# Two-layer attention on a picture: another order of the seven products, other halves of the channels, and a group norm by halves for the first batch

## The chip, the cores and the metric

The kernel runs on one core of a Trainium2 chip. Its time is device time in microseconds (us). TensorE (PE in the profile) multiplies matrices from SBUF into PSUM; VectorE (DVE), ScalarE (ACT) and GpSimd (POOL) work on whole tiles; SyncE (SP) issues most transfers. [...]

## The reference

The input is 8 pictures of 32 x 32 pixels with 512 channels, that is, per picture 1024 tokens of 512 values. Two layers follow each other, each with a residual:

```python
x = x + layer0(group_norm(x))   # 16 heads of 32: softmax(q k^T / sqrt(32)) v, then @ w_proj + b_proj
x = x + layer1(group_norm(x))   # 4 heads of 128: softmax((q k^T + position logits) / ...) v, then @ Wo
```

`group_norm` has 32 groups of 16 channels and takes mean and variance over a group's channels and all pixels. `layer0` gets q, k and v from one matrix w_qkv (512 x 1536), `layer1` from Wq, Wk and Wv (512 x 512 each). The position logits of layer 1 are products of q with two small tables of relative positions, one for the row and one for the column of a pixel, shifted so that each pair of pixels gets the logit of its distance. All is fp32.

## The kernel before, in words

**Tiling.** A picture's activations lie transposed in a `block` of SBUF: 128 partitions x 4 chunks of channels x 1024 tokens. `NB` = 512 tokens are a half (`NH` = 2), `NT` = 8 blocks of 128 tokens are the keys. PSUM has three pools: "ps" (4 banks, the scores of layer 0), "acc" (1), and "bank" with 3 buffers, which serve the products x, y, z, the position logits `pp`, and the scores and sums of layer 1.

**Projections.** Each of the eight 1024x512 by 512x512 projections per picture is Strassen's scheme in Winograd's form, with seven products instead of eight. The weights are cut into quarters (`quarter`, L120), the activations into a11, a12, a21, a22: the first index is the half of the tokens, the second the half of the channels. `forms` (L324 to L336) makes four sums on VectorE: s1 = a21 + a22 (L332), s2 = s1 - a11 (L333), s3 = a11 - a21 (L334, written over a21), s4 = a12 - s2 (L335). `Matrix.add_up` (L137, subtractions at L146) makes four such sums of the weights, once per matrix; `factor` (L152) names the weight that belongs to each product. `seven` (L341 to L396) runs the products; it is a generator that yields after each product. One call covers one unit (u = 0 or 1, a quarter of the 512 output columns in each half), so a projection is two units. In the list `fs` and in `ORDER` (L165) product number i is P(i+1):

```python
ORDER = [0, 5, 1, 4, 6, 2, 3]          # P1 P6 P2 P5 P7 P3 P4
return [a11, a12, s4, a22, s1, s2, a21]
```

P1 opens bank x and is copied by ACT (`p1`, L367). P6, which takes s2, opens y; DVE makes the snapshot a = y + p1 (L372). P2 adds onto x, which gives output quarter c11. P5 adds onto y, snapshot b = y + p1 (L380). P7, with s3, opens z and is copied by ACT (`p7`, L386). P3 adds onto y and gives c12; P4 adds onto z and gives c21, and c22 is b + p7. P5 can't start before a is read from y, nor P3 before b is. What becomes of the quarters is up to a sink: `Plain` (L398) writes them as q, k or v; `Onto` adds them onto the residual (L431, L436, L438) and, for the last projection, turns each finished block back (`ot`, L835) and sends it out (L840). `Stream` loads the weights of the next unit, product by product, on SyncE's queue, in the same queue as the outputs.

**Norm.** `statistics` (L241) takes mean and variance of a chunk into one small tile `mv`; `group_norm` (L254) turns it, averages over groups by a chain of some ten small DVE operations (L274 to L285), takes the power -0.5 on POOL (L289) and then scales four chunks (L292), yielding after the chain and after each second chunk.

**Attention.** `attention_0` (L519) goes over chunks m in the order 0, 2, 1, 3, halves h and key blocks j. A step is: scores into ps (L532), exp on ACT into one of two buffers `e` (L540), the product with v into acc (L551), and on DVE the addition of e onto `es` (L560 for the first, L562 after), which releases the e buffer. At the end of a half the sums over keys follow (L572) and `normalise` (L489): ACT copies su (L495), DVE turns it, takes reciprocals (L497 to L513), POOL multiplies (L517). `attention_1` (L637) does the same per head with its scores (L647), to which L648 adds the position logits from `posT`, in a bank; heads in order 0 to 3. `position_logits` (L594) makes posT in four steps: matmuls into `pp` (L608, L615), four ACT copies (L628) and four DVE subtractions (L633).

**What sets the order.** The program is written as generators, and they are merged by hand. In iteration b the steps of `attention_0` of picture b are interleaved with everything else (`side_by_side`, L862, which spreads a list of work by its cost over the attention's steps): the output projection of layer 0 for picture b-1 (`after_0`), the output projection of layer 1 for b-2 (`after_1`) with the norm of layer 1 for b-1, then `second` (L804: q, k, v of layer 1 and the position logits), `attention_1` of b-1 with the loading and norm of picture b+1, and `before_0` (q, k, v of layer 0 for b+1). `woven(main, side, start, gap, places)` (L850) inserts one step of `side` into `main` from step `start` on, at every `gap`. The norm of layer 1 is woven into `after_1` from product 3 at every third, the position logits into k and v from step 2, at three places per unit. A `hook` lets the four forms of the next output projection run inside the second unit of another projection, after its P3. In the first iteration there is no `after_1` to hide the norm of picture 0, so it runs with only attention beside it, each of its four steps with the cost ALONE. The last iterations have less and less work to merge, and after `attention_1` of picture 7 its output projection stands alone. A last few instructions (L979 to L985) set a flag if a softmax sum was out of bounds; another path of the program would then compute everything anew, which does not happen here.

## Time and profile before

Three runs took 3903.42, 3903.57 and 3906.62 us; the median is 3903.57 us. The profiled execution spans 3900.2 us. What matters in it:

| stretch of the span (us) | what runs | waits of TensorE of 0.25 us or more |
|---|---|---|
| 0 to 36 | loading, norm and first projection of picture 0 | 5.02 for x_rows, 9.32 for x_v, two short ones |
| 106 to 320 | attention_0 of picture 0 | eleven, together 13.5; three above 2 |
| 345 | output projection of picture 0 | 3.50 |
| 390 to 415 | norm of layer 1, picture 0 | 1.04, 7.58, 1.06, 1.04, 1.04 |
| 415 to 3200 | the iterations with full work | about 2.75 in each of five |
| 3214 to 3290 | last iteration with attention_0: output projections, norm | seven, together 7.6, the longest 2.66 |
| 3410 to 3460 | end of the last attention_0 | 0.40, 2.42, 2.58 |
| 3619 to 3866 | work of picture 6 and 7 that is left | 0.57, 1.74, 2.98, 0.32, 0.38, 0.75, 3.15 |
| 3890 to 3900 | outputs, flag | no matmul |

A row of the profile's groups names the line of the kernel, the engine, output and inputs, the number of instructions, their busy time and the mean of one, and then the idle time ahead of them with what ended it. A row of the waits names the waiting engine and line, then the releasing one, the total, how often and the longest. A stretch of the windows view gives busy time of each engine, and in PEclk the clock that was granted to TensorE, 1.00 being the full one; the mean over the run is 0.995.

### The profile page before, as it was taken

How to read it: one execution, taken by the hardware profiler on the slowest of the kernel's cores; microseconds unless marked ns; L12 is line 12 of the kernel's file. 1: busy time of each engine (PE TensorE's matmuls, PEld its weight loads, DVE VectorE, ACT ScalarE, POOL GpSimd, SP SyncE). 2: the span in 40 equal slices, each digit the busy share in tenths (PEclk: the TensorE clock that was granted, in tenths of full speed). 3: DMA queues.
4: the chain of work that ended last, by engine and by line, in shares of the span. 5: the costliest groups of instructions: out<-in, count | busy, mean ns of one | idle time of the engine just before them, and what ended most of it. 6: DMA issues, size and time to landing. Idle time of an engine off the chain costs nothing. (4 is left out here: it accounts for less than half of the span.)

```text
span 3900.2 us, 79833 instructions
## 1 busy us (share of the span) xinstructions
PE 3806.4 (98%) x34478; PEld 1370.9 (35%) x34478; DVE 2517.3 (65%) x2905; ACT 1725.1 (44%) x1767; POOL 621.7 (16%) x400
## 2 busy tenths in 40 slices
PE   8999899999999999999999999999999999999998
PEld 3222244232442224432343323433234332244353
DVE  5777675576745867468664686656865568754544
ACT  2554553445434454344544445344453445643132
POOL 1341001121101211012111121111210112011101
PEclk9999999999999999999999999999999999999999
DMA  5221120133202322023120241103311123110401
GB/s 172 86 95 51 40 61 3 39 117 70 59 5 63 107 57 55 12 91 84 46 55 17 92 94 40 44 24 97 88 45 32 31 92 69 32 63 18 124 17 23
DMA packets 482984, 234.73 MB, mean 60 GB/s; under 512 B 269600, under 2 KB 461376, under 8 KB 481600
## 3 DMA queue, kind: packets, MB, share of 16 engines
q1 hardware_dynamic: 470992, 213.74, 20.3%
q0 software_dynamic: 2608, 13.70, 1.0%
q8 instruction: 274, 4.49, 0.5%
q10 hardware_dynamic: 9024, 2.10, 0.3%
q14 instruction: 86, 0.70, 0.1%
HBM read 170.72 MB, written 58.72 MB: 59 GB/s over the span
## 5 line engine op out<-in xcount | busy, mean ns | idle before, releaser
L540 ACT ACTIVATE e<-ps 128x2048 f32<-128x2048 f32 x512 | 961.7, 1878 | 844.6 <-PE ps L532 605.9
L562 DVE TENSOR_TENSOR es<-es,e 128x2048 f32<-128x2048 f32 x384 | 890.8, 2320 | 400.2 <-ACT e L540 397.4
L532 PE MATMUL ps<-q,k 32*64 32x512 f32 x8192 | 577.2, 615 | 36.4 <-ACT e L540 36.3
L650 ACT ACTIVATE e<-ps 128x512 f32<-128x512 f32 x512 | 305.9, 598 | 585.9 <-PE ps L648 549.1
L551 PE MATMUL acc<-e,v 128*32 128x512 f32 x4096 | 547.1, 606 | 0.4 <-ACT su L495 0.4
L647 PE MATMUL ps<-q,k 128*128 128x512 f32 x1024 | 523.6, 593 | 0.4 <-DVE posT L633 0.4
L659 PE MATMUL acc<-e,v 128*128 128x512 f32 x1024 | 521.9, 592 | 0.0
L517 POOL TENSOR_TENSOR q<-q,su 128x512 f32<-128x512 f32 x128 | 214.3, 1674 | 1564.8 <-DVE su L513 1538.1
L670 DVE TENSOR_TENSOR es<-es,e 128x512 f32<-128x512 f32 x384 | 291.8, 760 | 264.0 <-ACT e L650 262.5
L648 PE MATMUL ps<-posT,sel 128*128 128x512 f32 x512 | 406.6, 794 | 0.0
L647 PEld LDWEIGHTS ps<-q,k 128*128 128x128 f32 x1024 | 193.6, 190 | 246.2 <-issue 240.6
L532 PEld LDWEIGHTS ps<-q,k 32*64 32x64 f32 x8192 | 120.4, 130 | 432.4 <-ACT e L540 217.0
L659 PEld LDWEIGHTS acc<-e,v 128*128 128x128 f32 x1024 | 193.1, 189 | 146.7 <-issue 105.0
L551 PEld LDWEIGHTS acc<-e,v 128*32 128x32 f32 x4096 | 81.5, 108 | 413.4 <-issue 365.8
L560 DVE TENSOR_TENSOR es<-e,e 128x2048 f32<-128x2048 f32 x64 | 174.7, 2730 | 39.7 <-ACT e L540 39.7
L497 DVE STREAM_TRANSPOSE tu<-su 128x512 f32<-128x512 f32 x128 | 90.6, 708 | 136.2 <-ACT su L495 136.0
L495 ACT COPY su<-sums 128x512 f32<-128x512 f32 x128 | 75.1, 586 | 151.3 <-PE sums L572 83.4
L648 PEld LDWEIGHTS ps<-posT,sel 128*128 128x128 f32 x512 | 97.3, 190 | 122.5 <-issue 122.5
L668 DVE TENSOR_TENSOR es<-e,e 128x512 f32<-128x512 f32 x64 | 44.2, 691 | 145.7 <-ACT e L650 145.7
L633 DVE TENSOR_TENSOR posT<-pp,posT 32x512 fp32r<-32x512 f32 x128 | 112.0, 875 | 32.2 <-ACT posT L628 30.8
L421 POOL TENSOR_TENSOR k<-b_k,p_k 128x512 f32<-128x512 f32 x32 | 51.2, 1599 | 477.0 <-ACT p_k L386 474.9
L628 ACT CAST posT<-pp 32x512 fp32r<-32x512 f32 x128 | 106.0, 828 | 45.2 <-PE pp L615 44.1
(195 smaller groups left out, 4510.1 us busy)
## 6 DMA issues: line engine op xcount, KB each, us to landing
w_qkv<-ws_qkv SPq DMA_DIRECT2D x168, 128.0 KB, 2.5
d<-x0T SPq DMA_DIRECT2D x32, 512.0 KB, 3.6
x1T<-d SPq DMA_DIRECT2D x32, 512.0 KB, 5.5
d<-x1T SPq DMA_DIRECT2D x32, 512.0 KB, 3.6
x2T<-d SPq DMA_DIRECT2D x32, 512.0 KB, 5.9
w_qkv<-in_L_conv_w_qkv SPq DMA_DIRECT2D x126, 128.0 KB, 2.2
out<-ot SPq DMA_DIRECT2D x240, 64.0 KB, 2.0
xs<-in_x SPq DMA_DIRECT2D x224, 64.0 KB, 2.6
```

Of the source, the lines that this page charges most:

```text
L517: nc.gpsimd.tensor_tensor(dst, dst, su, op=ALU.mult)
L532: nc.tensor.matmul(ps[some, r, :], k[m][rows, j * P + 64 * i : j * P + 64 * i + 64], q[m][rows, h * NB : (h + 1) * NB], start=True, stop=True,
L540: nc.scalar.activation(e, ps, AF.Exp, scale=D0 ** -0.5)
L551: nc.tensor.matmul(acc[r * D0 : (r + 1) * D0, :], v[:, j, c0 : c0 + D0], e[:, r, :], start=(j == 0), stop=(j == NT - 1),)
L560: nc.vector.tensor_add(state["esum"], state["first"], e)
L562: nc.vector.tensor_add(state["esum"], state["esum"], e)
L633: nc.vector.tensor_sub(rest, logits, greater)
L647: nc.tensor.matmul(ps, k[h][:, keys], q[:, h, queries], start=True, stop=False)
L648: nc.tensor.matmul(ps, sel_flat[:, keys], posT[:, h, queries], start=False, stop=True)
L650: nc.scalar.activation(e, ps, AF.Exp, scale=1.0 / math.sqrt(D1))
L659: nc.tensor.matmul(acc, v[:, j, h * D1 : (h + 1) * D1], e, start=(j == 0), stop=(j == NT - 1),)
L670: nc.vector.tensor_add(state["esum"], state["esum"], e)
```

## The change

The change aims at the places where a projection has to wait for the last piece of its input.

1. The halves of the channels are chunks 0, 2 and 1, 3 instead of 0, 1 and 2, 3 (activations and weight quarters alike). Since attention works in the order 0, 2, 1, 3, a11 and a21 are then complete when half of the chunks are. `attention_1` takes its heads in the same order.
2. The products run in the order P1, P7, P6, P2, P5, P4, P3. P7 needs only s3 = a11 - a21, which is now the first form and has a tile of its own; s1 is written over a21 instead. All three banks are open from P6 to P2. The quarter that is finished last is c12.
3. `forms_in_parts` is a generator. Hooks run one part each after P5, P4 and P3 of the second unit; before, all four forms ran in one hook.
4. The group norm takes a range of halves. For picture 0, layer 0 and layer 1, it runs by halves: the first half of the layer 1 norm is woven into the output projection, the second runs in the steps that cost ALONE. All other norms stay whole. They and the position logits are woven in one or two products later.
5. The weight sums of WQ0 and WK0 on DVE wait at the start for the last form of picture 0, and ACT does all copies of the turned input.

```diff
-        return w[:, k * HC : (k + 1) * HC, n * HN : (n + 1) * HN]
+        return w[:, k::2, n * HN : (n + 1) * HN]
+    IN_HALVES = [0, 2, 1, 3]
...
-    ORDER = [0, 5, 1, 4, 6, 2, 3]
+    ORDER = [0, 6, 5, 1, 4, 3, 2]
...
+    def forms_in_parts(x, name, got):
+        a11, a12 = x[:, 0::2, :NB], x[:, 1::2, :NB]
+        a21, a22 = x[:, 0::2, NB:], x[:, 1::2, NB:]
+        s3 = form(3)
+        nc.vector.tensor_sub(s3, a11, a21)
+        yield
+        nc.vector.tensor_add(a21, a21, a22)
+        s2 = form(2)
+        nc.vector.tensor_sub(s2, a21, a11)
+        yield
+        s4 = form(4)
+        last_form[0] = nc.vector.tensor_sub(s4, a12, s2)
+        got += [a11, a12, s4, a22, a21, s2, s3]
...
         p1 = snapshot("e1", f"p1_{name}")
         nc.scalar.copy(p1, x)
         yield HC
+        z = bank(f"z_{name}")
+        product(z, 6, True)
+        p7 = snapshot("e1", f"p7_{name}")
+        nc.scalar.copy(p7, z)
+        yield HC
         y = bank(f"y_{name}")
         product(y, 5, True)
...
         sink.middle(b)
-        yield HC
-        z = bank(f"z_{name}")
-        product(z, 6, True)
-        p7 = snapshot("e1", f"p7_{name}")
-        nc.scalar.copy(p7, z)
-        yield HC
-        product(y, 2, False)
-        sink.c12(y, p1)
-        if hook is not None:
-            hook()
+        next(hook, None)
         yield HC
         product(z, 3, False)
         sink.c21(z, a)
         sink.c22(b, p7)
+        next(hook, None)
+        yield HC
+        product(y, 2, False)
+        sink.c12(y, p1)
+        next(hook, None)
         yield HC
...
-            for cc in range(CC):
+            for cc in (0, 2, 1, 3):
                 part = xT[cc][:, h * NB : (h + 1) * NB]
-                if h == 0 or cc % 2:
-                    nc.scalar.copy(part, banks[cc])
-                else:
-                    nc.vector.tensor_copy(part, banks[cc])
+                nc.scalar.copy(part, banks[cc])
...
+        for half in range(2):
+            put_away(st, xT, (half,), "0_0")
+            run(group_norm(st, xT, (half,), "0_0"))
+            next(sums)
+        run(sums)
...
-            keys_and_values, position_logits(q, posT, b), 2, len(ORDER), (0, 1, 2)
+            keys_and_values, position_logits(q, posT, b), 4, len(ORDER), (0, 1, 2)
...
-        m.add_up(nc.vector, nc.gpsimd, keep=True)
+        with tc.issue_after(last_form[0].ins):
+            m.add_up(nc.vector, nc.gpsimd, keep=True)
...
-                rest.append(woven(later(after_1, b - 2, past), norm, 3, 3))
+                rest.append(woven(later(after_1, b - 2, past), norm, 4, 2))
...
-                rest.append(chain([ALONE], (cost + ALONE for cost in norm), marked()))
-                total += 4 * ALONE
+                norms = [norm_1(b - 1, last, (half,)) for half in range(2)]
+                rest.append(woven(after_0(b - 1, last), norms[0], len(ORDER) + 3, 2))
+                rest.append(chain([ALONE], (cost + ALONE for cost in norms[1]), marked()))
+                total += 3 * ALONE
```

## The prediction

> **What bounds the kernel now.** I read the shares of busy time first, then the waits of TensorE, then its granted clock by stretch, and last the records inside the longest waits.

> ```profile
> PE 3806.4 (98%) x34478; PEld 1370.9 (35%) x34478; DVE 2517.3 (65%) x2905; ACT 1725.1 (44%) x1767; POOL 621.7 (16%) x400
> ```

> TensorE (PE) works 3806.4 of 3900.2 us; the next engine, VectorE (DVE), has a third of its time free. The diff adds and removes no matmul, so all it can win is the idle 93.8 us and time lost to a lowered clock. Adding up the idle time ahead of each PE record gives 83.6 us up to the last matmul and 10.2 us behind it.

> ```profile
> PE ps L532 <- ACT e L540: 36.3, 30, 7.6
> PE y_wo L312 <- DVE a_wo L372: 11.2, 9, 1.7
> PE x_v L312 <- issue: 9.3, 1, 9.3
> PE y_wp L312 <- DVE f_ao L333: 3.5, 1, 3.5
> PE y_wo L312 <- DVE f_ao L333: 3.1, 1, 3.1
> PE x_q L312 <- DMA w_q<-in_L_conv_Wq: 3.0, 1, 3.0
> PE ps L647 <- DVE posT L633: 0.4, 1, 0.4
> ```

> Columns: total us, times, longest. Nearly all waits are for a result of DVE or ACT that is late once, not for one that is always too slow.

> ```profile
> 350.00:400.00 50.00, 41.60 (x436) 10.17 (x424) 40.02 (x50) 21.44 (x15) 8.85 (x8) 0.94 0.23 78
> 450.00:850.00 400.00, 400.00 (x3592) 150.50 (x3588) 252.74 (x293) 184.80 (x197) 47.88 (x33) 1.00 0.17 50
> 343.60:350.30 6.70, 4.85 (x28) 0.91 (x28) 4.72 (x5) 0.00 (x0) 0.30 (x1) 0.50 0.01 3
> 394.80:404.90 10.10, 4.45 (x32) 0.87 (x40) 10.03 (x9) 3.75 (x2) 0.00 (x0) 0.50 0.00 0
> 3655.50:3660.00 4.50, 4.47 (x44) 1.75 (x48) 0.68 (x1) 0.59 (x1) 0.00 (x0) 1.00 0.87 246
> ```

> After the times come busy time of PE, weight load, DVE, ACT and POOL, then PEclk. A whole iteration in the middle (450 to 850) has no idle PE; the waits sit in the first and last iteration and where two stages meet. Behind some waits the clock is 0.50, so the PE work there costs double. Why the 7.58 us wait at 400 arises, DVE shows:

> ```profile
> 393.74 2.26 DVE L292 TENSOR_SCALAR x1T<-x1T,back,rstd 128x1024 f32<-128x1024 f32 x3 [1.16 <-POOL rstd L289]
> 395.91 2.28 DVE L560 TENSOR_TENSOR es<-e,e 128x2048 f32<-128x2048 f32 x1
> ```

> ```profile
> 398.29 1.88 ACT L540 ACTIVATE e<-ps 128x2048 f32<-128x2048 f32 x1 [7.81 <-DVE es L560]
> ```

> The addition that frees an exp buffer stands behind the norm's chain and its scalings, so ACT waits 7.81 us, and PE for ACT. At the end of the kernel the chain of waits reads:

> ```profile
> 3860.22 1.26 POOL q L517
> 3861.49 0.02 issue
> 3861.51 2.28 DVE f_ao L332
> 3863.79 0.02 issue
> 3863.82 1.24 DVE f_ao L333
> 3865.05 0.04 issue
> 3865.10 2.79 PE y_wo L312 x16
> ```

> P6 needs s2 (L333), which needs the last normalised block.

> [...] five half-clock stretches ahead of the end follow waits of 9.3, 3.5, 7.6, 2.66 and 3.15 us, while the 2.98 us wait at 3655.5 shows 1.00 in the row above. So shortening a wait from 3.5 to 1 us saves more than the wait. [...] the kernel uses 4 (scores) + 1 + 3, so the third open product takes the last. [...]

> **The change part by part.** Prices: a product 1.72 us of PE; score group and value group about 1.05 us each; a form (128x1024) 1.2 us of DVE, in places 2.3; an exp 1.88; an es addition 2.3; a scaling 0.75 to 0.83.

> *First projection of batch 0.* x_v starts at 25.55. DVE no longer does the eight weight sums (L146, 8 x 0.67 = 5.3 us) between the statistics; four of them, 2.65 us, lie ahead of the first scaling. A first norm over two chunks has 1.5 us of scaling instead of 2.98 before P1. But all statistics still come first, POOL's power L289 still queues behind POOL's own sums, and the eight sums now stand before the snapshot a_v, for which P5 waits. Between 0 and 5 us gained; I take 2.5.

> *Output projection of batch 0 (345).* Heads run in chunk order 0, 2, 1, 3, and halves are now chunks 0,2 and 1,3; so P1 and P7 need only blocks finished long before. P7 (1.72) fills the wait for s2: PE would reach P6 near 344.4 against s2 at 345.4. The 3.5 us wait falls to about 1.1, and the 6.7 us at half clock, with 4.85 us of work, go: 2.4 + 2.4 = 4.8. I take 4.5.

> *Norm of batch 0, layer 1 (390 to 415).* Waits of 1.04 + 7.58 + 1.06 + 1.04 + 1.04 = 11.8, plus 2.3 for the 4.45 us of work at half clock, 14 in all. Half of the norm moves into the projection, the rest has two scalings instead of four, and P1 and P7 no longer wait for it. The chain of small operations (389 to 393.7) is paid twice, but once under matmuls. I leave 6.5 as waiting: gain 7.5; ends 3 and 11.

> *Later norms and forms (five iterations).* Each now loses about 2.75 us: 1.0 to 1.3 (ps waits for exp), 1.42 (y_wo for a_wo, behind two es additions of 4.65 us), 0.3. Scalings go in two pairs of 1.5 instead of one block of 2.98, the four forms in three parts instead of 5 us at once. 1.1 stays: gain 5 x 1.65 = 8; ends 0 and 13.

> *Last loaded iteration (3214 to 3290).* The same norm and forms without other work to hide them: 7.6 us of waits and 1.5 of half clock; gain 4.5, ends 0 and 8.

> *Position logits.* They start after P5, P4, P3 instead of P2, P5, P7, so posT is done two products (3.4 us) later. Behind the last pp there remain P4, P3, a score and value group and L647, about 6 us, against four copies (4 x 0.83) and a subtraction (0.88), with an exp or es addition ahead: 4.2 to 8 us. What waits is L648[...]. Per batch 0 to 2 us; I take 0.4, for eight batches 3 lost; ends 0 and 14.

> *Three open banks.* P1, P7 and P6 open x, z and y before any closes. The next x follows P3 directly but takes the bank that c11 freed; the next y comes two products after c12's read. That covers 0.7 us of reading unless an es addition stands ahead. Cost 0 to 0.3 us in each of 128 units; I take 5 us in all.

> *Tail (3600 on).* y_wo for a_wo (0.57 + 1.74) shrinks by 1.3; the w_q load stands behind the last outputs on SyncE's queue, and with one block (c12) last instead of two it goes out some 1.5 us earlier; at 3860 to 3869 the waits of 0.75 and 3.15 and the 1.65 of half clock (3.3 us of work) lose 3, since P1 and P7 go ahead of P6; the end after the last matmul has one block to add, turn and store, not two: 0.7. Together 6.5; ends 2 and 9.

> The 13.5 us of waits between 106 and 320 I leave: exp and es waits in a first iteration whose order changes little; within 3 either way. The sparser DVE rows added (22, small) cost nothing of their own: matmuls hide them.

> Sum: 2.5 + 4.5 + 7.5 + 8 + 4.5 + 6.5 - 3 - 5 = 25.5. 3903.6 - 25.5 = **3878**.

> **The rivals.** (A) *The waits come back*: posT costs 1.5 us in each batch (12, not 3) and the steady iterations gain nothing: 25.5 - 9 - 8 = 8.5, so 3895; with a little less elsewhere, no change. For it: eight waits of one kind are easily made, and DVE is at 46.4 of 50 us in 850 to 900. Against: there the new order spreads DVE's work. (B) *Slower*: three banks leave no spare one, and each of 128 units waits 0.3 us (38 instead of 5): 25.5 - 33 = -8; with posT as in A, 3921. For it: y_wo already waits for a_wo nine times, where a DVE addition stands ahead of the read. Against: in 450 to 850 PE does not wait at all with the same distance, one product, between P6, P2 and P5. (C) *More*: steady, last and first iterations lose all waits named and no half clock stays: another 15, so 3863.

> **How the numbers follow.** Forecast 0.60, A 0.17, B 0.12, C 0.11. The range takes the forecast, C, and A down to no change at 3900; B is left out. 0.2% is 7.8 us: faster is forecast, C and a third of A, 0.76; same 0.13, slower 0.11.

> **What would show it.** In the changed kernel's profile: y_wp and the last y_wo waits for s2 near 1 us with the clock at 1.00 behind them; the wait at 400 below 3 us; fewer than nine waits of y_wo for a_wo; ps waiting for posT in several batches, under 1 us each. I am wrong if posT waits exceed 2 us, if x, y or z products wait for their banks' readers in many units, or if the new snapshot p7 and the sums delay ACT or a_v for longer than the waits removed.

## The result: slower by half a per cent

The changed kernel takes 3922.81 us (median of four runs, 3921.88 to 3922.93) against 3903.49 us before: ratio 1.0048, 95% interval 1.003 to 1.0065. The prediction said 3878.

Read first what TensorE (PE) did, from the first part of the changed kernel's page:

```profile
PE 3825.9 (98%) x34478; PEld 1368.8 (35%) x34478; DVE 2531.8 (65%) x2921; ACT 1725.9 (44%) x1769; POOL 552.8 (14%) x402
```

The span grew by 20.7 us (3900.2 to 3920.9), the idle time hardly: 84.1 us up to the last matmul against 83.6, and 10.9 behind it against 10.2. It is the busy time that grew, by 19.5 us, with the same 34478 matmuls. PE's busy time inside the half-clock stretches ahead of the last matmul is 43.5 us after and 19.4 us before. In one of these stretches (PEclk 0.50) the 16 matmuls of a product took 3.39 us (y_q at 3666.20, up to the next product at 3669.59), behind it 1.72 (3674.15 to 3675.87). At that ratio about half of the busy time there is lost, and about 12 of the 19.5 us stand under the clock in this trace. The other 7 us left no idle record; that they are short stalls inside groups of matmuls is not shown.

That does not make the clock the cause. Of the four executions three had a mean granted clock of 0.993; the fourth had 0.995, as the kernel before, and took 3922.93 us, no less than the others. And the run f4 below takes 3923.2 us with no half clock in any of the five full iterations: its trace has 3817.4 us of busy time and 92.0 us idle up to the last matmul. Where the clock stayed up, the time showed as waiting.

The waits of PE in the changed kernel:

```profile
PE ps L557 <- ACT e L565: 25.4, 26, 3.1
PE sums L597 <- DVE es L587: 10.7, 7, 2.0
PE x_v L324 <- issue: 5.4, 1, 5.4
PE y_wp L324 <- DVE b_wp L409: 5.1, 5, 1.0
...
PE y_wo L324 <- DVE a_wo L401: 4.7, 2, 3.1
PE acc L684 <- ACT e L675: 4.5, 6, 0.9
PE y_q L324 <- DMA w_q<-in_L_conv_Wq: 4.2, 1, 4.2
...
PE ps L673 <- DVE posT L658: 1.9, 1, 1.9
PE z_v L324 <- DVE v L439: 1.8, 1, 1.8
...
PE y_wp L324 <- DVE f_ao L351: 1.0, 1, 1.0
```

The waits that the change aimed at did shrink: x_v from 9.3 to 5.4, y_wp for s2 from 3.5 to 1.0, the 7.6 us one is gone. Rows that weren't there, or were small, have taken their place: sums for es (one of 2.6 before), y_wp for b_wp, acc for exp, scores for posT (0.4 before), z products for the reader of c12.

Where in the program the time went, by the start of the first score matmul of each picture in both traces (and, at the end, by the first matmul of a stage):

| stretch | before | after | difference |
|---|---|---|---|
| to attention_0 of picture 1 | 335.8 | 331.0 | -4.8 |
| to attention_0 of picture 2 | 469.5 | 462.4 | -7.2 |
| five full iterations, to picture 7 | 2366.2 | 2389.4 | +23.3 |
| to the output projection of layer 0, picture 7 | 418.1 | 416.7 | -1.3 |
| the two output projections behind it | 50.8 | 52.0 | +1.2 |
| q, k, v of layer 1 and logits, picture 7, alone | 85.3 | 91.9 | +6.6 |
| attention_1 of picture 7, alone | 131.7 | 135.9 | +4.2 |
| last output projection and end | 42.9 | 41.6 | -1.3 |

An iteration lasts 477.9 us instead of 473.2. One of them, taken apart in the same way: +1.2 in the output projection of layer 0 (wp), +2.1 from the start of that of layer 1 (wo) to the layer 1 projections, -0.6 up to attention_1, +1.7 in attention_1, +0.3 in before_0. The +2.1 can be seen on DVE, with an addition that POOL does meanwhile:

```profile
871.16 1.22 DVE L347 TENSOR_TENSOR f_xn<-x1T 128x1024 f32<-128x1024 f32 x1
872.29 0.69 DVE L401 TENSOR_TENSOR a_wo<-y_wo,p_wo 128x512 f32<-128x512 f32 x1
872.90 1.22 DVE L349 TENSOR_TENSOR x1T<-x1T 128x1024 f32<-128x1024 f32 x1
874.15 2.19 DVE L351 TENSOR_TENSOR f_xn<-x1T 128x1024 f32<-128x1024 f32 x1
876.26 2.28 DVE L587 TENSOR_TENSOR es<-es,e 128x2048 f32<-128x2048 f32 x1
```

```profile
873.06 2.19 POOL L456 TENSOR_TENSOR x2T<-x2T,a_wo 128x512 f32<-128x512 f32 x1 [9.69 <-DVE a_wo L401]
```

```profile
878.68 1.06 PE L597 MATMUL sums<-es,ones 128*32 128x512 f32 x8 [2.00 <-DVE es L587]
```

```profile
879.80:883.10 3.30, 3.30 (x24) 0.60 (x28) 1.92 (x4) 1.93 (x2) 1.26 (x1) 0.50 0.50 75
```

Three forms of the next projection stand ahead of the last es addition: its e was there at 870.82 us (an exp of 1.88 us from 868.94), and it began at 876.26, behind them (one of them, beside POOL's addition, took 2.19 us instead of 1.22); the sums of the attention wait 2.00 us for it; and for 3.4 us behind the wait PE works at half clock. Before, this place had two waits of 1.0 to 1.3 and 1.42 us, and the clock stayed at 1.00.

The run f4, whose edit lies elsewhere, shows what the half clock cost here. It has the same wait at the full clock, and then another one, 12 us later:

```profile
881.89 1.06 PE L597 MATMUL sums<-es,ones 128*32 128x512 f32 x8 [2.00 <-DVE es L587]
...
893.61 1.12 PE L557 MATMUL ps<-q,k 32*64 32x512 f32 x16 [1.43 <-ACT e L565]
```

Its iterations last 477.6 us, those of the changed kernel 477.9. The slow matmuls fill time in which PE would have waited for exp; what is lost from wo to attention_1 is 1.5 us with the half clock and 1.3 without it.

### The profile page after: what moved, and what is told of

It reads as the page before. It is cut to its first block, busy times and chain, and to the rows that moved or that the text cites. A ratio compares the mean times of both kernels' runs of the same rounds, so it can differ in the third digit from the quotient of the medians.

```text
span 3920.9 us, 79829 instructions
## 1 busy us (share of the span) xinstructions
PE 3825.9 (98%) x34478; PEld 1368.8 (35%) x34478; DVE 2531.8 (65%) x2921; ACT 1725.9 (44%) x1769; POOL 552.8 (14%) x402
## 4 chain that ended last, share of the span: by engine, by line
PE 81%; DVE 11%; ACT 3%; issue 3%; DMA 1%; POOL 1%; SPq 0%; DVEq 0%; ACTq 0%; POOLq 0%
PE ps L557 11%; PE acc L684 11%; PE ps L672 11%; PE acc L576 10%; PE y_k L324 4%; PE y_q L324 4%; PE y_v L324 4%; DVE es L587 4%; PE ps L673 3%; PE x_q L324 3%; PE z_k L324 3%; PE z_v L324 3%; PE z_q L324 3%; PE x_k L324 2%; PE x_v L324 2%
## 5 line engine op out<-in xcount | busy, mean ns | idle before, releaser
L557 PE MATMUL ps<-q,k 32*64 32x512 f32 x8192 | 578.8, 618 | 25.5 <-ACT e L565 25.4
L542 POOL TENSOR_TENSOR q<-q,su 128x512 f32<-128x512 f32 x128 | 203.2, 1587 | 1658.8 <-DVE su L538 1652.3
L446 POOL TENSOR_TENSOR k<-b_k,p_k 128x512 f32<-128x512 f32 x32 | 40.9, 1277 | 407.7 <-DVE b_k L409 382.4
```

The lines of the kernel that those rows point to most:

```text
L542: nc.gpsimd.tensor_tensor(dst, dst, su, op=ALU.mult)
L557: nc.tensor.matmul(ps[some, r, :], k[m][rows, j * P + 64 * i : j * P + 64 * i + 64], q[m][rows, h * NB : (h + 1) * NB], start=True, stop=True,
```

## The experiments

In short, with what one full iteration (a fifth of the stretch from picture 2 to picture 7) lasts longer than in the kernel before, where it lasts 473.2 us:

| run | what differs | us | one iteration |
|---|---|---|---|
| before | | 3903.5 | 0 |
| changed | | 3922.8 | +4.7 |
| e1_norm_33 | changed, norm at 3, 3 | 3932.3 | +5.5 |
| e2_pos_3 | changed, logits from 3 | 3949.9 | +9.2 |
| e4_norm_33_pos_3 | both | 3960.8 | +10.7 |
| e3_old_order | changed, old product order | 3903.9 | +1.4 |
| f1_p3_last | e3, P4 ahead of P3 | 3951.1 | +5.5 |
| f3_forms_held | changed, forms behind b | 3916.0 | +4.3 |
| f4_subs_together | changed, subtractions together | 3923.2 | +4.4 |
| f6_old_order_s2_first | e3, old order of the forms | 3894.2 | -0.1 |
| g1_s3_pool | changed, s3 on POOL | 3932.7 | +5.4 |
| g2_old_order_s3_pool | f6, s3 on POOL | 3909.2 | +1.0 |
| g4_old_order_pos_4 | f6, logits from 4 | 3908.9 | +1.0 |
| g5_forms_in_one_hook | changed, one hook | 3924.0 | +4.6 |
| h1_no_s3 | changed, s3 left out | 3920.5 | +3.5 |
| h2_norm_43 | changed, norm at 4, 3 | 3923.9 | +4.7 |
| h3_mixed | f6, new order in two places | 3891.0 | -0.1 |
| i1_two_banks | f6, P7 fourth, c12 last | 3919.5 | +3.1 |

**First guesses: the two times of weaving.** My first theories were that the norm ends too early (N) and that the logits come too late (P); the rival (O) was the order of the products itself.

```diff
-                rest.append(woven(later(after_1, b - 2, past), norm, 4, 2))
+                rest.append(woven(later(after_1, b - 2, past), norm, 3, 3))
```

> The changed kernel with one number pair set back: the norm of layer 1 woven into the second output projection from product 3 at every third, not from 4 at every second. Theory N (the earlier end of the norm lets the forms of the next stage stand ahead of the es addition that the sums wait for: 2.00 us of wait and 1.65 us of half clock in each of five iterations): those waits go, waits of 1.0 to 1.4 us as in the kernel before come back, so about 5 x 2.3 = 11 us less, 3911. Theory P (late position logits) and theory O (the order of the products, three open banks): the steady iterations stay at 477.9 us, 3923.

Measured: 3932.3 us, ratio 1.0074 (1.0057 to 1.009). Slower than the changed kernel. The edit wasn't the return it looked like: in the new order step 3 lies ahead of P5, so the norm moved ahead of P5. In the first full iteration its scalings ran at 848 to 854 us around an es addition, and the scores waited 3.63 us for exp.

```diff
-            keys_and_values, position_logits(q, posT, b), 4, len(ORDER), (0, 1, 2)
+            keys_and_values, position_logits(q, posT, b), 3, len(ORDER), (0, 1, 2)
```

> The changed kernel with the position logits woven from step 3 instead of 4, so after P2, P5 and P4 instead of P5, P4 and P3: one product earlier. Theory P: the wait of scores for posT at the start of attention_1 (with the value product's 0.85 us behind it, 1.7 us longer than before in each iteration, 3.5 us at picture 7) goes: about 5 x 1.5 + 3.5 = 11 us less, 3912. Theories N and O: no change at that place, 3923.

Measured: 3949.9 us (1.0106 to 1.014). The logits can't go earlier in this order: with x, z and y open, pp behind P2 asks for the bank of x, and the trace shows pp waiting for the ACT copy of c11 (1.0 us in all) and y products waiting for a (2.6 us in all), and 4.6 us more in each iteration than in the changed kernel. Two of its five iterations have the half clock behind the sums' wait and three don't; all five last 482.4 to 482.6 us, so here too the half clock cost next to nothing.

> Both edits of the two runs with norm and position logits set back, everything else as changed. If N and P are both right and independent: 11 + 11 less, about 3901, with the gain of the first 400 us kept. If they share one cause (DVE busy at the same moment) less than the sum, 3908. Theory O: 3923.

Measured: 3960.8 us (1.0132 to 1.0166). The two losses add up. But both edits moved the work to a place of their own, so neither tested its theory: N comes again in h2, P in g4.

**The product order.** The run e3 puts the order back, with the place of the logits that goes with it, and leaves all else changed:

```diff
-    ORDER = [0, 6, 5, 1, 4, 3, 2]
+    ORDER = [0, 5, 1, 4, 6, 2, 3]
...
-            keys_and_values, position_logits(q, posT, b), 4, len(ORDER), (0, 1, 2)
+            keys_and_values, position_logits(q, posT, b), 2, len(ORDER), (0, 1, 2)
```

> The changed kernel with the products in the order of before (P1, P6, P2, P5, P7, P3, P4) and the position logits from step 2 with it; halves, forms in parts and norms stay as changed. Theory O: the waits of z products for the reader of c12 (0.88 + 0.88 + 1.80 us at picture 7) and of y_wp for b_wp (5 x 1.01) go and the early waits return only in part (345 us: +2.4, tail: +3): about 3916. Theory N: still 3.6 us per iteration lost at the sums, only the position part (11 us) comes back: 3915 with the 345 wait and tail added. Theory P alone gives the same. What tells them apart is where in the iteration the time comes back.

Measured: 3903.9 us, ratio 1.0004 (0.9995 to 1.0012). Of 19 us, all come back with the order and the earlier logits. Against the kernel before it still loses 1.4 us per iteration between x_q and attention_1. The next run asks whether that is s3, which is now made ahead of s2:

```diff
-        s3 = form(3)
-        nc.vector.tensor_sub(s3, a11, a21)
-        yield
-        nc.vector.tensor_add(a21, a21, a22)
-        s2 = form(2)
-        nc.vector.tensor_sub(s2, a21, a11)
+        s1 = form(3)
+        nc.vector.tensor_add(s1, a21, a22)
+        yield
+        s2 = form(2)
+        nc.vector.tensor_sub(s2, s1, a11)
         yield
+        nc.vector.tensor_sub(a21, a11, a21)
         s4 = form(4)
```

> The kernel with the old order of products, halves and norms as changed, and the forms in the old order too (s1, s2, then s3 and s4), so that P6, again the second product, gets s2 without waiting for s3. In the run with the old order the stretch from x_q of layer 1 to attention_1 was 1.4 us longer than before in each iteration, with a wait of 1.39 us of the scores for exp. If s3 ahead of s2 on DVE is what costs that: 6 x 1.4 = 8 less than 3903.9, so 3895, faster than both kernels. If not: 3904.

Measured: 3894.2 us, ratio 0.9982 (0.9976 to 0.9989). As expected: the 1.4 us are gone from each iteration, and the gain of the first 800 us (8.0 us in this trace) is kept to the end.

**Which part of the order?** Two things go together in it: P7 is early, so three banks are open, and P4 comes ahead of P3, so c12 is last.

```diff
-    ORDER = [0, 5, 1, 4, 6, 2, 3]
+    ORDER = [0, 5, 1, 4, 6, 3, 2]
```

> Between the changed kernel and the one with the old order: P7 stays fifth as before, but P4 comes ahead of P3 (P1, P6, P2, P5, P7, P4, P3; position logits from step 2). At most two banks are open until P7, as before. Theory O1 (it is P7 in second place, with three open banks and the forms needed early, that costs 19 us against the old order): about 3904. Theory O2 (it is that c12 comes last, so that its reader stands between P3 and the next products): about 3915 to 3923.

Measured: 3951.1 us (1.0107 to 1.0141), beyond both. Here P4 follows P7 directly and can't start before ACT has copied z; before_0 alone is 3.75 us longer in each iteration. So its time doesn't tell the two apart. Its trace says something about one place: although c12 is last in it too, DVE adds es ahead of the forms where wo meets x_q, as in the old order, and the only wait there is one of 1.18 us (y_wo for a_wo). The next run has a product between them and two banks:

```diff
-    ORDER = [0, 5, 1, 4, 6, 2, 3]
+    ORDER = [0, 5, 1, 6, 4, 3, 2]
```

> The kernel with the old order and s2 first, with the products in the order P1, P6, P2, P7, P5, P4, P3: c12 is last as in the changed kernel, but x is closed before z is opened (two banks open), P4 doesn't follow P7 directly, and the position logits start from step 2. Theory O1 (three open banks and the late logits they force): only the 1.2 us of P3's wait for b is left in each iteration, about 3894 + 6 = 3900. Theory O2 (c12 last is what costs): as in the changed kernel, 3915 to 3923.

Measured: 3919.5 us (1.0027 to 1.0055), 25 more than f6. So three open banks aren't needed for a loss of this size: an order with two banks and early logits, but c12 last and P7 fourth, has one too. Its trace has no wait for b in wp and none at attention_1 in the full iterations, but again one of 2.30 us (scores for exp) where wo meets x_q. No wait of 0.25 us or more follows that one for 80 us, and here the half clock does cost: the three iterations that have it behind the wait last about 477.0 us, the other two 475.4. It also has 11.3 us more while layer 1's projections of picture 7 run alone, where P3 waits for b (1.0 to 1.7 us in each unit) and P4 for the copy of P7.

**The late logits by themselves,** in the old order:

```diff
-            keys_and_values, position_logits(q, posT, b), 2, len(ORDER), (0, 1, 2)
+            keys_and_values, position_logits(q, posT, b), 4, len(ORDER), (0, 1, 2)
```

> The kernel with the old product order and s2 first, with the position logits as late as in the changed kernel (from step 4: after P7, P3 and P4). Theory L (the 1.7 us at the start of each attention_1 and the 3.5 us at picture 7 come from the place of the logits alone): 5 x 1.7 + 3.5 = 12 more, 3906. Theory O2 (they come from c12 being last, whose reader frees the bank of the first scores): unchanged, 3894.

Measured: 3908.9 us (1.0009 to 1.0025), 14.7 more than f6; in the trace the 0.85 us wait of acc for e at the start of attention_1 is back, and the stretch of picture 7 alone is 4.8 us longer. So in the old order the late logits by themselves cost 10 (trace) to 15 us (medians), about 1 us of it in each full iteration. Bringing the subtractions together doesn't help:

```diff
-                if i % 2:
-                    yield 0
+            yield 0
...
-            keys_and_values, position_logits(q, posT, b), 4, len(ORDER), (0, 1, 2)
+            keys_and_values, position_logits(q, posT, b), 4, len(ORDER), (0, 1)
```

> The changed kernel, with the four subtractions of the position logits in one step after P4 instead of two after P4 and two after P3; the matmuls of the logits stay where they are, so no bank is asked for earlier. Theory P' (posT is late because its last two subtractions stand behind P3's reader on DVE): the 1.7 us at the start of each attention_1 and the 1.87 us wait at picture 7 shrink by half or more: about 7 us less, 3916. If posT is late for the ACT copies or for the place of pp itself: 3923.

Measured: 3923.2 us (1.0042 to 1.0075), no change against the changed kernel. It isn't the place of the last two subtractions. (This is the run without half clock in its full iterations.)

**The place where wo meets the layer 1 projections.** First the forms are held back; then s3 is given to POOL (`third` is POOL for layer 1's input); then it is left out.

```diff
-        fs = forms(st.pop("x1"), f"xn1_{b}")
+        with tc.issue_after(half_done[0].ins):
+            fs = forms(st.pop("x1"), f"xn1_{b}")
```

> The changed kernel, with the forms of the next stage's input (the 1.22, 1.22 and 2.19 us of subtractions at 871 to 876) held back on DVE until the snapshot b of the last unit of wo is made, so behind the last es addition instead of ahead of it. Theory F (these forms delay the es addition, the sums wait 2.00 us for it, and a half-clock stretch of 3.4 us follows): the sums' wait and the half clock go, 5 x (2.0 + 1.6) = 18 us less, minus up to 1 us per iteration if P7 then waits for s3: 3905 to 3910. If the place of the forms is not the cause: 3923.

Measured: 3916.0 us (1.0023 to 1.0052), 7 less than the changed kernel and not 15. The sums' wait goes, and a wait of 2.30 us of the scores for exp comes at x_q: the forms now stand ahead of another es addition. The wait had moved, not gone. As in i1, no such wait follows it for 80 us, and the half clock costs: the four iterations with half clock there last 477.8 us, the first, without it, 476.2.

```diff
-        nc.vector.tensor_sub(s3, a11, a21)
+        third.tensor_tensor(s3, a11, a21, op=ALU.subtract)
```

> The changed kernel with s3 of the input of the layer 1 projections computed on POOL, which is idle there, instead of on DVE; nothing is held back. Theory D (where the second output projection meets the projections of layer 1, DVE has about 2 us more to do than the time allows; the order only chooses which wait shows it, and in the changed kernel it is one wait of 2.0 us that halves the clock): with 1.2 us taken off DVE the wait falls below 1 us and the half clock goes, 5 x (1.2 + 1.6) = 14 less, 3909; if POOL takes so long that P7 waits, less. If the wait is one of order only: 3923.

Measured: 3932.7 us (1.0063 to 1.0094), 10 more. POOL's subtraction and the scalings on DVE at the same time read:

```profile
1346.44 2.38 POOL L347 TENSOR_TENSOR f_xn<-x1T 128x1024 f32<-128x1024 f32 x1 [1.55 <-PE z_wo L324]
```

```profile
1346.67 3.42 DVE L303 TENSOR_SCALAR x1T<-x1T,back,rstd 128x1024 f32<-128x1024 f32 x2
```

In the changed kernel the same two scalings, with POOL quiet, are:

```profile
865.15 1.50 DVE L303 TENSOR_SCALAR x1T<-x1T,back,rstd 128x1024 f32<-128x1024 f32 x2
```

DVE lost 1.92 us beside 2.38 us of POOL, more than the 1.22 that were taken from it. This run couldn't test theory D, since it freed no time. The same edit in f6:

> The kernel with the old product order and s2 first, with the same s3 on POOL (there P7 is fifth and can wait for it). Theory D: the waits of 1.0 and 1.42 us per iteration (scores for exp, y_wo for a_wo) shrink by 1.2 us in all, 5 x 1.2 = 6 less than 3894: 3888. If they stand ahead of the place where DVE gets the time back: 3894.

Measured: 3909.2 us (1.0007 to 1.0023), 15 more than f6; in the traces 5.1 of it in the full iterations, but 4.9 already ahead of picture 1, where the edited line hasn't run yet. So the next run leaves the work out instead, for pictures 1 to 7:

```diff
-        nc.vector.tensor_sub(s3, a11, a21)
+        s3 = form(3) if third else a11
+        if third:
+            nc.vector.tensor_sub(s3, a11, a21)
...
-        fs = forms(st.pop("x1"), f"xn1_{b}")
+        fs = forms(st.pop("x1"), f"xn1_{b}", b == 0)
```

> The changed kernel without the subtraction s3 = a11 - a21 for the input of the layer 1 projections of pictures 1 to 7 (P7 multiplies a11 itself there, which leaves out that part of the computation); nothing else is moved. Theory D (DVE owes about 2 us at this place): 1.2 us less DVE work takes the sums' wait from 2.0 to 0.8 and the half clock of 3.4 us goes: 5 x (1.2 + 1.6) = 14 less, 3909. Theory F2 (not the amount but the place of the forms ahead of the es addition): the other two forms still stand there, 3.4 us, and the wait falls by 1.2 as well, but no further; then h2_norm_43 tells.

Measured: 3920.5 us (1.003 to 1.0061). The half clock is gone from all five iterations, and the sums' wait too; the scores wait 1.85 and 1.43 us there, against 0.59, 2.00 and 1.43 in f4, the run to compare with, since it has no half clock either. An iteration is 1.15 us shorter than in the changed kernel, for 1.22 us of DVE work left out. Theory D falls in the form that gave a number, which counted 1.6 us of half clock for lost; that DVE's work sets the pace at this place agrees with the run.

```diff
-                rest.append(woven(later(after_1, b - 2, past), norm, 4, 2))
+                rest.append(woven(later(after_1, b - 2, past), norm, 4, 3))
```

> The changed kernel with the norm woven at every third product as in the kernel before, from product 4 on, so still behind the snapshot b (the run with 3 and 3 had put it ahead of b). Theory F2: the norm then ends three products later, the forms can't stand ahead of the last es addition, the 2.0 us wait and the half clock go: up to 18 less, 3905. Theory D: the wait only moves, as in the run with the forms held back: 3916 to 3923.

Measured: 3923.9 us (1.0035 to 1.0065), and the same sequence on DVE: forms, then es, a wait of 2.01 us. The list of DVE came out as in the changed kernel although the steps were woven in further apart. F2 wasn't tested by it, because the forms didn't move.

**The hooks in parts.**

```diff
         sink.middle(b)
-        next(hook, None)
...
         sink.c22(b, p7)
-        next(hook, None)
...
         sink.c12(y, p1)
-        next(hook, None)
+        run(hook)
```

> The changed kernel with all parts of the forms in the hook after the last product, as before, instead of one part after each of P5, P4 and P3. Theory H (the forms of the next projection stand ahead of the snapshot b of wp on DVE, for which P3 waits 1.01 us in each iteration): that wait goes, 5 x 1.2 = 6 less, 3917, unless the forms then come too late for P7. If not: 3923.

Measured: 3924.0 us (1.004 to 1.007). The wait of y_wp for b_wp stays at 1.02 us; the forms weren't what stands ahead of b.

**A version that beats both.** This run has the new order only in the two projections where the kernel before had P6 waiting for s2:

```diff
+        early = name[:5] in ("wp_0_", f"wo_{B - 1}_")
+        if early:
+            z, p7 = seventh()
+            yield HC
```

> The kernel with the old order and s2 first, and the changed order (P7 second, s3 first, c12 last) only in the output projection of layer 0 for picture 0 and that of layer 1 for picture 7, the two places where P6 waits for s2 (3.5 and 3.1 us, both with half clock behind). If the early P7 pays where nothing else runs on DVE: 2.4 + 2.4 at 345 us and 2 + 1.7 at the end less, 3886. If it costs as much there as in the steady iterations: 3894.

Measured: 3891.0 us, ratio 0.9967 (0.9955 to 0.9979), faster than before by 13 us and the lowest median of all; 3 less than f6, of 8 expected, and the two intervals overlap. In the traces it gains on f6 6.0 us from picture 1 to picture 2 and 1.4 at the end, where the two projections lie, and is 4.4 us longer ahead of picture 1, where neither does. Its waits for s2:

```profile
PE y_wo L324 <- DVE f_ao L352: 2.4, 1, 2.4
...
PE y_wp L324 <- DVE f_ao L352: 1.0, 1, 1.0
```

The wait at 345 us is what the prediction had for P7 filling it (1.1); at the end it is 0.7 us shorter than before, as in the changed kernel.

## Why the prediction was wrong, point by point

- *First projection, 2.5*: right. The wait of x_v fell from 9.3 to 5.4 us, and attention_0 of picture 0 started 2.1 us earlier.
- *Output projection of picture 0 and norm of layer 1, 4.5 + 7.5*: right in mechanism and nearly in size. The two stretches to attention_0 of picture 2 gained 12.0 us, with the 2.5 above 14.5 were predicted. (Up to picture 1 the gain varies: 1.5 to 4.8 us in the ten traces that begin in this way.) y_wp waited 1.01 us for s2, as worked out, with no half clock behind it; at 371 a wait of 2.19 us for a_wp was new, with half clock behind it. Behind the norm 5.6 us of waits were left, where I had left 6.5.
- *Later norms and forms, 8 gained*: **this step failed.** From wo to attention_1 each iteration lost 1.5 us instead of gaining 1.65. The scalings came in pairs, as I said (the row at 865.15), but the forms did not come in parts at this place: the hooks split the forms of the output projections, while `second` still makes those of the layer 1 projections in one go, in both kernels. They moved ahead of the last es addition. At the full clock (f4) the waits there are 0.59, 2.00 and 1.43 us, against 1.0 and 1.42 before; in the changed kernel half-clock work takes the place of the last one. I had read that DVE is busy 46.4 of 50 us there and took it only as a point for a rival.
- *Position logits, 3 lost, between 0 and 14*: **mis-sized.** By themselves they cost 10 to 15 us in the old order (g4 against f6). I took 0.4 us per picture from an estimate of 4.2 to 8 us for the way to posT against 6 us of cover; it was the upper end that came.
- *Three open banks, 5 lost, at most 38*: **mis-sized, and put in the wrong places.** It was not 0 to 0.3 us in every unit but a few long waits: y_wp 1.01 us for b in each iteration, where wp became 1.2 us longer, and z products 0.88, 0.88 and 1.80 us for the reader of c12 when the projections of picture 7 run alone. i1, with two banks, loses 16 us against 19. So the number of banks is not what decides; that it is the distance of the reader a product waits for is my reading, and no run isolates it.
- *Last loaded iteration, 4.5*: 1.3 gained. *Tail, 6.5*: **the sign was wrong**, since I looked only at waits that existed. The last output projection and the end gained 1.3, with the wait for s2 at 2.40 us, not near 1, and half clock behind it; the stages alone in front of it lost 10.8: w_q 4.20 instead of 2.98 us, now for P6's weights, the z waits, 1.87 us for posT, and half clock behind the first and the last of them.
- *The half clock*: I counted what would go (2.4, 2.3, 1.5, 1.65 us), not what might come: ahead of the end there are twelve stretches instead of five, 47.8 us instead of 34.1. And I counted all of it as time lost, which held in f3 and i1, where no wait followed (1.6 us), and not in the changed kernel's full iterations (0.3 us against f4).
- *Rivals*: B was the right side with 3921 for 3923, and with a chance of 0.12. That the number fits is luck: its reason, 0.3 us for each unit from three banks, is not what the runs show. My point against it didn't hold either: 450 to 850, where PE never waits, is not the whole iteration that I called it. An iteration is 473 us long, and its waits lie in the part left out.

What stays open: why the new order puts the forms ahead of an es addition where wo meets the layer 1 projections, with one wait of 2.0 to 2.3 us (also in f3 and i1), while the old order has two shorter ones. The runs moved it (f3), made it larger (g1) or split it (h1), and none of those with P7 early reached the list of DVE that the old order has. c12 last is not enough for it, since f1 has c12 last and the old list there; whether the earlier P7 alone does it wasn't tested. Nor was what makes y_wp wait for b: the forms in the hook don't (g5).

## What to carry to other kernels

When a new order of work removes a long wait in one place, apply it in that place: here the edits gained 12 us in the first two stretches, where projections waited for their input, and lost 35 in others, most of it where little had waited. Look for the stretches where a second engine is nearly full, because there moving or splitting work can merely move a wait (f3), and what shortened an iteration was less work (h1). If a busy engine's busy time grows with the same number of instructions, look at its clock, but then at an execution in which the clock stayed up: only what that one saves is what the clock cost (here 0.3 us an iteration, f4).

## What the runs showed of the hardware

```profile
876.33:879.74 3.41, 1.41 (x20) 0.25 (x18) 3.38 (x4) 0.00 (x0) 0.00 (x0) 1.00 0.00 0
879.74:883.16 3.42, 3.42 (x26) 0.66 (x28) 2.01 (x4) 1.99 (x2) 1.26 (x1) 0.50 0.49 75
```

```profile
877.10:880.51 3.41, 2.78 (x28) 0.65 (x20) 3.38 (x3) 0.55 (x2) 1.36 (x1) 1.00 0.08 22
880.51:883.93 3.42, 2.04 (x25) 0.42 (x25) 3.12 (x4) 0.59 (x1) 0.19 (x1) 1.00 0.02 5
```

- So a repeated wait is not repeated evidence. The changed kernel's iteration of 477.9 us is 140.0 steps of 3.413 us, and the steps ahead of its five half-clock stretches have nearly the same busy share of PE (0.412 or 0.413); that all five waits were followed by half clock is one case, not five.
- Three operations of DVE that started while POOL was at an elementwise one took longer by about nine tenths of the time that they overlapped: 1.92 us of 2.15 (g1, the scalings above), 1.10 of 1.22 (g1, an es addition of 3.38 us instead of 2.28), 0.97 of 1.10 (the changed kernel, the form at 874.15); POOL's spans are rough. Not every operation did: in the kernel before, two additions onto x2T (L436, at 873.68 and 874.28 us) started beside an addition of POOL (873.49, 1.42 us) and took 0.68 us each, against 0.69 without POOL (870.88). What tells them apart is not shown. With s3 moved to POOL two kernels were 10 and 15 us slower (g1 and g2, medians).
- Neither idle time nor busy time alone told here what a wait cost. With idle time within 1.3 us of the kernel before, the changed kernel was 20.7 us longer; f4, just as long, shows about 8 us more as idle and 8 us less as busy.
